# Where row degrees are summed, when one operand tile is loaded, and when projected rows are left for the next layer, in a two-layer Strassen-Winograd graph kernel

## The chip, the cores and the metric

The kernel runs on one core of a Trainium2 chip. The core has a matrix engine (TensorE, PE in the profile; its weight loads are listed as PEld), a vector engine (VectorE, DVE), an activation engine (ScalarE, ACT), GpSimd (POOL) and a sync engine (SyncE, SP). Each works through its own instructions in order, and they wait for each other by semaphores. In this kernel SP issues the large loads, POOL the stores and the loads of rows. The metric is the device time of one execution in microseconds; smaller is better.

## The reference, cut to what matters

```python
def _L0(cur, inc0):                       # N = 4096 rows, D = 512
    head = (inc0 > 0).astype(...)         # head: 1 where the adjacency is positive
    head = head / maximum(sqrt(sum(head * head, axis=-1)), 1e-12)
    inc = inc0 + head
    return (inc @ cur) / sum(inc, axis=-1)
def _L1(X, A, W):
    A2 = A + eye(N)
    dscale = diagonal(A2) ** -0.5
    return relu((dscale[:, None] * A2 * dscale[None, :]) @ (A2 @ X @ W.T))
x = layernorm(x + _L0(x, adj))
x = layernorm(x + _L1(x, adj, L1_gnn_W))
```

All is float32. The adjacency is 4096 x 4096. There are three large products with it: one in layer 0 and two in layer 1. The degree of a row in layer 0 is the row's sum of `inc`, that is the row sum of the adjacency plus the row sum of the normalised head; with c positive entries in the row, the latter is c/sqrt(c) = sqrt(c).

## The kernel before, in words

Every large product is done by a Winograd form of Strassen's scheme: the left factor is cut into four quarters A11, A12, A21, A22, the right one into B11, B21, B22 and one more, and seven products of sums of quarters (with A sums S1 to S4 and B sums T1 to T4) take the place of eight. The seven accumulate in seven PSUM banks; the eighth bank is a spare.

*First stage (layer 0).* Rows are taken in 16 pairs j (row block j and row block j + 16, of 128 rows each). A pair has four chunks c of the contraction (NC = 4), each a tile `a` of 128 x 2048, loaded by SP (`load_chunk`, L308, three buffers) two chunks ahead. For the chunk after the one being multiplied, DVE forms the sums with the head's mask (`prepare1`: L416, L435, L442 and `add_up`, L167 to L170). `multiply1` (L472) then issues 4 x 7 matmuls. B tiles hold W = 258 columns, 256 of features and two of ones, so that products A11, A12 and S1 also give row sums, the degrees; the other four are 256 wide (H). The first pair is done without the scheme (`multiply_plain`, L485). At the start of a pair, `combine` reads the last pair's banks: ACT copies two of them (L503, L507), DVE does the rest (L504 to L513), among it the two columns of `deg`.

The head needs 1/sqrt(count) of a row before its mask. So natural rows of the adjacency go by once more: `load_natural` (SP, L367) brings tiles `nat` of 128 x 512, five buffers, 16 tiles to a pair; `count(k)` has ACT apply Sign to k of them with a sum beside it (L332) and asks for k more loads. `count` is called after each chunk's multiply, with the numbers of a tuple by chunk. `spread(j + 1, 0)`, in the second chunk, reduces the counts on DVE and takes the root on ACT (L336). `layer0` (second chunk) divides by the degree, adds x and normalises (ACT L153 and L162, DVE L159), `operands` (third chunk) forms T sums and POOL stores B operands for the next stage in DRAM (`outer_b[2]`, L540 to L542).

*Second and third stage (layer 1: k = 2 and 3).* Now the order is written out as 224 `steps` (k, s, p, kk): half s of the left rows, product p of an outer seven (`ORDER`), and kk of eight blocks. Each step is seven matmuls of 512 columns (`multiply2`, L278; an inner level of the same scheme), A tiles come two to three steps ahead by SP (`load`, L213 and L217), B operands two groups ahead, a group being two steps (`load_b_up_to`, L250, tile `tr`, three buffers), and DVE sums both (`add_up`, `sum_b` L257 to L259). After eight steps `outer` drains the banks (L684 to L692). The last pair of the first stage is still given to `layer0` in step 0 and `operands` in step 1.

When a half of stage 2 is done, its columns are multiplied with W.T by `project`, two blocks at kk = 2 and 4 of a product, each with seven small products placed between the seven matmuls of a step (`between`, by slot 0 to 6). Each of these uses the spare bank and is copied out by ACT at once (L766 and L768), so the next one waits for this copy. After the seven, DVE forms the results `z` and the difference `t`, and `leave_operands` scales them on ACT by dscale or its negative (L816) and stores them as B operands of stage 3 from POOL (L819, L826); the second half (h = 0) adds T2, T3 and T4 to what the first (h = 1) has written.

Of the kernel before, what the change touches and what calls it, by code (L numbers as in the profile page):

```python
# [13 lines left out]
P = 128  # L14
# [12 lines left out]
def tile_adj_resnorm_d2(  # L27
# [44 lines left out]
    NC = NP // CK  # L72
    CW = CK * P
    W = H + 2
    NAT = 512
    NT = N // NAT
    NQ = NB // 4
# [117 lines left out]
    going = []  # L195
    queue, pairs, later, deferred, raises = [], [], [], [], []

    def fresh():
# [102 lines left out]
    chunks, sums, slots, counts, scale, natural = {}, {}, {}, {}, {}, {}  # L301
    xr = {}

    mask = w1_pool.tile([P, 2, CW], F32, name="mask", bufs=1)
# [65 lines left out]
    def count(times):  # L370
        for _ in range(times):
            if not waiting:
                return
            (j, h, t), nat = waiting.pop(0)
            if j not in counts:
                counts[j] = w1_pool.tile([P, 2, NT], F32, name="cnt")
            signs(nat, nat, counts[j][:, h, t:t + 1])
            load_natural()

    def spread(j, part):  # L380

        if part == 0:
            n = w1_pool.tile([P, 2], F32, name="n", bufs=2)
            nc.vector.tensor_reduce(n, counts.pop(j), axis=mybir.AxisListType.X, op=ALU.add)
            to_scale(n, n)
            scale[j] = n
        elif part == 1:
            n = scale.pop(j)
            nc.vector.tensor_scalar(n, n, EPS, None, op0=ALU.max)
            nc.vector.reciprocal(n, n)  # L390
            d = w1_pool.tile([P, 2, P], F32, name="d", bufs=1)
            for h in range(2):
                nc.vector.tensor_scalar(d[:, h, :], ident, n[:, h:h + 1], None, op0=ALU.mult)
            scale[j] = d
        elif part == 3:

            n = scale.pop(j)
            nc.vector.tensor_scalar(n, n, EPS, None, op0=ALU.max)
            nc.vector.reciprocal(n, n)
            row = dram.tile([P, 2], F32, name=f"sc{j}")  # L400
            nc.gpsimd.dma_start(out=row, in_=n)
            s = w1_pool.tile([P, P, 2], F32, name="sc")
            nc.gpsimd.dma_start(out=s.rearrange("p i h -> p (i h)"), in_=row.rearrange("i h -> (i h)").partition_broadcast(P))
            scale[j] = s.rearrange("p i h -> p h i")
        else:
# [50 lines left out]
        add_up(sums[n], chunks[n])  # L456

    def multiply1(n, acc, then=None):
        c = n % NC
        a, s = chunks.pop(n), sums.pop(n)  # L460
        for i in range(CK):
            kk = c * CK + i
            b = slots[kk]
            cols = slice(i * P, (i + 1) * P)
            if then is not None and i == CK - 1:
                then()
            for m, (left, right, w) in enumerate((
                (a[:, A11, cols], B11, W), (a[:, A12, cols], B21, W), (s[:, S2, cols], T2, H),
                (s[:, S1, cols], T1, W), (s[:, S3, cols], T3, H), (s[:, S4, cols], B22, H),
                (a[:, A22, cols], T4, H),  # L470
            )):
                nc.tensor.matmul(acc[m][:, 0:w], left, b[:, right, 0:w], start=(kk == 0), stop=(kk == NP - 1))  # L472
# [15 lines left out]
    def take(h, acc):  # L488

        y = row_tile("z", 2)  # L490
        nc.scalar.copy(y[:, 0:H], acc[0][:, 0:H])
        nc.scalar.copy(y[:, H:D], acc[1][:, 0:H])
        nc.scalar.copy(deg0[:, h:h + 1], acc[0][:, H:H + 1])
        return y

    def combine(acc):

        q1, q2, q6, q5, q7, q3, q4 = acc
        top, low = row_tile("z", 2), row_tile("z", 2)
        p1, p5 = row_tile("p1", 1)[:, 0:W], row_tile("p5", 1)[:, 0:W]  # L500
        u2, u3 = row_tile("u2", 1)[:, 0:H], row_tile("u3", 1)[:, 0:H]
        deg = small.tile([P, 2], F32, name="deg", bufs=2)
        nc.scalar.copy(p1, q1[:, 0:W])  # L503
        nc.vector.tensor_add(top[:, 0:H], q2[:, 0:H], p1[:, 0:H])  # L504
        nc.vector.tensor_add(deg[:, 0:1], q2[:, H:H + 1], p1[:, H:H + 1])
        nc.vector.tensor_add(u2, q6[:, 0:H], p1[:, 0:H])
        nc.scalar.copy(p5, q5[:, 0:W])  # L507
# [5 lines left out]
        nc.vector.tensor_copy(deg[:, 1:2], p5[:, H:H + 1])  # L513
        return top, low, deg

    def load_rows(j):
        for h in range(2):
# [3 lines left out]

    def layer0(j, C):

        rd = small.tile([P, 2], F32, name="rd", bufs=2)
        nc.vector.reciprocal(rd, C[2])
        stats = []
        for h in range(2):
            y = C[h]
            nc.vector.scalar_tensor_tensor(y, y, rd[:, h:h + 1], xr.pop(h), op0=ALU.mult, op1=ALU.add)
            stats.append(statistics([y]))  # L530
        for h in range(2):
            normalise(C[h], *stats[h])
            nc.gpsimd.dma_start(out=x1_rows[j + h * NP], in_=C[h])

    def operands(j, C):

        top, low, _ = C
# [15 lines left out]
    deg0 = small.tile([P, 2], F32, name="deg", bufs=2)  # L553
# [70 lines left out]
    prepare1(NC)  # L624
    build_last(4)
    multiply_plain(1, 3, low)
    C = top, take(1, low), deg0
    load_rows(0)

    for n in range(NC, NP * NC):  # L630
        j, c = divmod(n, NC)
        if c == 0:
            if j > 1:
                C = combine(acc)
            acc = [bank(m) for m in range(7)]
        if n + 2 >= NP * NC:
            load_up_to(n + 2 - NP * NC)
# [10 lines left out]
            for g in range(5, NP // 2):  # L648
                build_last(g)
        multiply1(n, acc, (lambda: spread(j + 1, 2)) if scales and j == 1 else None)  # L650
        count(((6, 6, 4, 6) if j == 1 else (6, 0, 4, 6))[c])
        if j == 1 and c == 1:
            nc.vector.tensor_scalar(dscale, dscale, 1.0, None, op0=ALU.add)
            nc.scalar.activation(dscale, dscale, AF.Sqrt)
# [46 lines left out]
    def outer(k, p, acc):  # L701
# [26 lines left out]
        else:  # L728
# [6 lines left out]
                into(c21)  # L735
                deferred.append(lambda: add(c11, c21))
            elif p == 6:
                by_way(lambda i, y: add(c21[:, i, :], y))
                deferred.append(lambda: add(c12, c21))
            elif p == 7:  # L740
                by_way(lambda i, y: add(c21[:, i, :], y))
                deferred.append(lambda: less(c22, c22, c21))
            else:
                by_way(lambda i, y: nc.vector.tensor_sub(c21[:, i, :], y, c21[:, i, :]))

    def blocks(h, s):

# [2 lines left out]
    def project(h, s, n, first):  # L750
# [51 lines left out]
        t = row_tile("t", 1, (P, 4, H))  # L802
        for r in range(2):
            nc.vector.tensor_sub(t[:, 2 * r, :], z[r][:, 0:H], z[r][:, H:D])
        for r in range(2):
            leave_operands(h, r * NQ + s * SB + n, z[r], t[:, 2 * r, :], t[:, 2 * r + 1, :])
        yield

    def leave_operands(h, j, z, t, m):

        b = j + h * NP

        def scaled(o, y, by=dscale):
            nc.scalar.activation(o, y, AF.Copy, scale=by[:, b:b + 1])  # L816

        def put(op, y, **how):
            nc.gpsimd.dma_start(out=in_outer(3, j, slice(op, op + 1)), in_=y.unsqueeze(1), **how)  # L819
# [75 lines left out]
    def finish(h, items, acc):  # L895
# [14 lines left out]
        def put(i, op):  # L910
            y = row_tile("y", 2)
            op(y)
            nc.vector.tensor_sub(c21[:, i, :], y, c21[:, i, :])

        def turn(t):
            j, r, cols = items[t]
# [70 lines left out]
    load_up_to(2)  # L987
    load_b_up_to(2)
    sum_b(0)
    C = combine(acc)  # L990
    prepare(1)
    PF = 1
    for n, (k, s, p, kk) in enumerate(steps):
# [104 lines left out]
```

## Time and profile before

| what | value |
|---|---|
| median of 3 runs | 2283.88 us (2283.74 to 2288.45) |
| the profiled execution's own time | 2284.03 us |
| its span, first to last instruction | 2282.1 us |
| mean granted TensorE clock | 0.998 |
| busy: PE / DVE / ACT / POOL | 2255.1 / 1854.4 / 417.3 / 383.3 us |
| first stage by pairs (L472) | from 73.5 to 803.5 us |
| stages 2 and 3 (L278, then L908) | from 803.5 us to the tail at about 2265 us |

In the lists below, a row of a group names the line, the engine, the operation, `tile written<-tiles read`, and the shapes; a row of a timeline begins with its start and its duration in microseconds, and a bracket at its end gives the idle time before it and what ended it. A row of the waits gives the total in microseconds, how often, and the longest. `q` is a PSUM bank, `nat` a tile of natural rows, `tr` the loaded B operands, `ob` and `oa` operands in DRAM. One float32 matmul appears as two records on PE.

### The profile page before, as it was taken

What the parts mean: (1) busy time and instruction counts of PE and PEld (TensorE: products, weight loads), DVE (VectorE), ACT (ScalarE), POOL (GpSimd) and SP (SyncE); (2) the same over time, 40 slices, a digit from 0 to 9 for tenths busy, and PEclk for the clock granted to TensorE, in tenths of its full rate; (3) what the DMA queues carried; (4) which work ended last, traced back from release to release, by engine and by line L of the source; (5) the groups of instructions that cost most, each with busy time, mean ns of one, the idle gap of its engine ahead of it and who ended that gap; (6) DMA issues with size and microseconds to landing.
All of it is one profiled execution on the core that took longest, in us unless ns stands there. A gap on an engine that the chain in (4) does not pass through costs nothing.

```text
span 2282.1 us, 22004 instructions
## 1 busy us (share of the span) xinstructions
PE 2255.1 (99%) x7359; PEld 1380.3 (60%) x7359; DVE 1854.4 (81%) x2619; ACT 417.3 (18%) x991; POOL 383.3 (17%) x548
## 2 busy tenths in 40 slices
PE   8999999999999999999999999999999999999997
PEld 6888888888888844444555444555544444444443
DVE  6988988988988777788876778887666788776788
ACT  4333223332232000000222100122110011100013
POOL 0111112211111110001333300232320000100013
PEclk9999999999999999999999999999999999999999
DMA  9788777878777576575767857576785676766573
GB/s 330 274 287 262 260 233 270 272 262 270 238 240 239 187 266 259 198 283 184 270 240 227 262 209 271 191 283 261 209 256 218 220 258 241 253 238 227 209 269 117
DMA packets 155936, 555.80 MB, mean 244 GB/s; under 512 B 17920, under 2 KB 32272, under 8 KB 117424
## 3 DMA queue, kind: packets, MB, share of 16 engines
q1 hardware_dynamic: 114624, 417.38, 51.6%
q0 software_dynamic: 41200, 137.03, 18.2%
q8 instruction: 58, 0.95, 0.2%
q14 instruction: 54, 0.44, 0.1%
HBM read 434.78 MB, written 119.55 MB: 243 GB/s over the span
## 4 chain that ended last, share of the span: by engine, by line
PE 89%; DVE 5%; DMA 3%; ACT 2%; issue 1%; POOL 0%; SPq 0%; DVEq 0%; ACTq 0%
PE q L278 55%; PE q L472 27%; PE q L766 3%; PE q L485 2%; DMA nat<-adj 2%; DVE s L167 1%; PE q L908 1%; PE q L844 1%; DVE s L169 0%; ACT z L816 0%; ACT nat L332 0%; DVE a L442 0%; DVE mask L435 0%; ACT t L816 0%; DVE ts L257 0%
## 5 line engine op out<-in xcount | busy, mean ns | idle before, releaser
L278 PE MATMUL q<-s,ts 128*128 128x512 f32 x1326 | 612.2, 592 | 0.1
L472 PE MATMUL q<-b,s 128*128 128x256 f32 (+1 forms) x1920 | 454.4, 379 | 0.0
L278 PEld LDWEIGHTS q<-s,ts 128*128 128x128 f32 x1326 | 251.6, 190 | 299.1 <-issue 268.3
L167 DVE TENSOR_TENSOR s<-a 128x1024 f32<-128x1024 f32 x236 | 290.2, 1230 | 161.4 <-PE q L278 131.3
L472 PEld LDWEIGHTS q<-b,s 128*128 128x128 f32 x1920 | 363.1, 189 | 53.1 <-DVE z L510 0.5
L472 PE MATMUL q<-b,a 128*128 128x258 f32 (+1 forms) x1440 | 352.5, 380 | 0.7 <-ACT p L503 0.6
L278 PE MATMUL q<-a,tr 128*128 128x512 f32 x692 | 329.4, 592 | 1.8 <-DMA a<-adj_r 1.8
L472 PEld LDWEIGHTS q<-b,a 128*128 128x128 f32 x1440 | 272.5, 189 | 40.9 <-ACT p L503 1.5
L278 PE MATMUL q<-s,tr 128*128 128x512 f32 x442 | 225.7, 592 | 0.0
L278 PEld LDWEIGHTS q<-a,tr 128*128 128x128 f32 x692 | 129.5, 190 | 145.1 <-issue 138.9
L332 ACT ACTIVATE nat<-nat,tiny 128x512 f32<-128x512 f32 x240 | 170.9, 714 | 235.9 <-DMA nat<-adj 235.7
L278 PE MATMUL q<-a,ts 128*128 128x512 f32 x346 | 176.8, 592 | 0.0
L169 DVE TENSOR_TENSOR s<-a,s 128x512 f32<-128x512 f32 x236 | 167.7, 711 | 8.1
L170 DVE TENSOR_TENSOR s<-a,s 128x512 f32<-128x512 f32 x236 | 167.3, 709 | 8.0
L442 DVE TENSOR_TENSOR a<-a,mask 128x1024 f32<-128x1024 f32 x123 | 150.7, 1225 | 6.6 <-DVE mask L435 0.5
L435 DVE SCALAR_TENSOR_TENSOR mask<-a,sc 128x1024 f32<-128x1024 f32 (+2 forms) x129 | 154.1, 1196 | 2.1
L278 PEld LDWEIGHTS q<-s,tr 128*128 128x128 f32 x442 | 84.0, 190 | 92.1 <-issue 84.6
L684 ACT COPY p<-q 128x512 f32<-128x512 f32 x27 | 15.6, 577 | 631.5 <-PE q L278 631.5
L278 PEld LDWEIGHTS q<-a,ts 128*128 128x128 f32 x346 | 65.7, 190 | 83.0 <-issue 76.1
L425 POOL DMA_DIRECT2D oa<-sr x64 | 57.7, 902 | 283.8 <-DVE sr L416 181.6
L873 POOL DMA_DIRECT2D out<-o x24 | 13.1, 547 | 507.8 <-ACT o L162 507.8
L278 PE MATMUL q<-r,tr 128*128 128x512 f32 x192 | 92.7, 593 | 0.0
(193 smaller groups left out, 2129.4 us busy)
## 6 DMA issues: line engine op xcount, KB each, us to landing
a<-adj_r SPq DMA_DIRECT2D x112, 1024.0 KB, 6.6
a<-oa SPq DMA_DIRECT2D x80, 1024.0 KB, 5.3
nat<-adj SPq DMA_DIRECT2D x240, 256.0 KB, 7.4
a<-adj_q SPq DMA_DIRECT2D x60, 1024.0 KB, 6.2
tr<-ob SPq DMA_DIRECT2D x112, 512.0 KB, 4.0
oa<-sr POOLq DMA_DIRECT2D x64, 512.0 KB, 7.2
oa<-r POOLq DMA_DIRECT2D x32, 1024.0 KB, 9.2
y<-x POOLq DMA_DIRECT2D x64, 256.0 KB, 7.2
```

Of the source, the lines that this page charges most:

```text
L167: nc.vector.tensor_add(s[:, S3:S1 + 1, :], a[:, A11:A22 + 1, :], a[:, A21, :].unsqueeze(1).to_broadcast([P, 2, w]))
L169: nc.vector.tensor_add(s[:, S2, :], a[:, A11, :], s[:, S1, :])
L170: nc.vector.tensor_add(s[:, S4, :], a[:, A12, :], s[:, S2, :])
L278: nc.tensor.matmul(acc[m], left, right, start=(kk == 0), stop=(kk == NQ - 1))
L332: nc.scalar.activation(y, a, AF.Sign, bias=tiny, scale=2.0 ** 64, accum_out=accum)
L425: nc.gpsimd.dma_start(out=dst, in_=sr.rearrange("p m (k i) -> p (m k) i", i=P))
L435: nc.vector.scalar_tensor_tensor(m, v, 0.0, s.unsqueeze(1).to_broadcast(list(v.shape)), op0=ALU.is_gt, op1=ALU.mult)
L442: nc.vector.tensor_add(z, z, y)
L472: nc.tensor.matmul(acc[m][:, 0:w], left, b[:, right, 0:w], start=(kk == 0), stop=(kk == NP - 1))
L485: nc.tensor.matmul(y[:, 0:w], left, slots[kk][:, op, 0:w], start=(kk == 0 and left is k1), stop=(kk == NP - 1 and left is k2))
L766: nc.tensor.matmul(ps, left[:, e, :], wt[:, right, e, :], start=(e == 0), stop=(e == 1))
L844: nc.tensor.transpose(ps[:, at + i * P:at + (i + 1) * P], C_of[3][h][d // 2][:, 2 * r + d % 2, cols], ident)
```

## The change

There are three parts.

1. *Degrees.* From pair 4 on (SUMMED = 4) the three products that gave row sums are 256 wide. Instead, `count` has ACT run over each `nat` tile twice: a copy in place with a sum beside it, then Sign as before. `spread` reduces the sums too (`deg`), and adds the root `n`, which is sqrt(count). `combine` no longer forms `deg` for these pairs. The tiles counted after each chunk are (6, 6, 5, 6) for pair 1 and (5, 4, 5, 2) for the others, where they were (6, 6, 4, 6) and (6, 0, 4, 6).
2. *One load.* At step 1 `load_b_up_to` is not called any more; at step 3 it asks for two groups.
3. *Leaving operands.* For the first of two projected blocks, `leave_operands` is called inside the next step, its two row blocks in slots 2 and 4; for the second it is called at the end of the step as before. T2 and T4 are stored with their sign turned, so that T2 goes with T3 (h = 1) or with T4 (h = 0) in one DMA from one tile. For the two row blocks of a projected block together, six scalings and eight DMAs become four and six where h = 1, and eight scalings and ten DMAs become six and eight where h = 0. The signs are put right where products 6 and 4 are added.

```diff
+    SUMMED = 4
...
             if j not in counts:
                 counts[j] = w1_pool.tile([P, 2, NT], F32, name="cnt")
+                if j >= SUMMED:
+                    totals[j] = w1_pool.tile([P, 2, NT], F32, name="tot")
+            if j >= SUMMED:
+                nc.scalar.activation(nat, nat, AF.Copy, accum_out=totals[j][:, h, t:t + 1])
             signs(nat, nat, counts[j][:, h, t:t + 1])
             load_natural()
...
             to_scale(n, n)
+            if j >= SUMMED:
+
+                deg = degrees[j] = w1_pool.tile([P, 2], F32, name="deg", bufs=3)
+                nc.vector.tensor_reduce(deg, totals.pop(j), axis=mybir.AxisListType.X, op=ALU.add)
+                nc.vector.tensor_add(deg, deg, n)
             scale[j] = n
...
+        wide = W if j < SUMMED else H
...
-                (a[:, A11, cols], B11, W), (a[:, A12, cols], B21, W), (s[:, S2, cols], T2, H),
-                (s[:, S1, cols], T1, W), (s[:, S3, cols], T3, H), (s[:, S4, cols], B22, H),
+                (a[:, A11, cols], B11, wide), (a[:, A12, cols], B21, wide), (s[:, S2, cols], T2, H),
+                (s[:, S1, cols], T1, wide), (s[:, S3, cols], T3, H), (s[:, S4, cols], B22, H),
...
-        count(((6, 6, 4, 6) if j == 1 else (6, 0, 4, 6))[c])
+        count(((6, 6, 5, 6) if j == 1 else (5, 4, 5, 2))[c])
...
-                by_way(lambda i, y: add(c21[:, i, :], y))
+                by_way(lambda i, y: nc.vector.tensor_sub(c21[:, i, :], c21[:, i, :], y))
...
-                by_way(lambda i, y: nc.vector.tensor_sub(c21[:, i, :], y, c21[:, i, :]))
+                by_way(lambda i, y: less(c21[:, i, :], y, c21[:, i, :]))
...
-        for r in range(2):
-            leave_operands(h, r * NQ + s * SB + n, z[r], t[:, 2 * r, :], t[:, 2 * r + 1, :])
+        leaving.extend(lambda r=r: leave_operands(h, r * NQ + s * SB + n, z[r], t[:, 2 * r, :]) for r in range(2))
...
         if h:
-            scaled(m, second, nscale)
-            scaled(z, z)
-            scaled(t, t)
+            scaled(z, dscale)
+            scaled(t, nscale)
             nc.gpsimd.dma_start(out=in_outer(3, j, slice(B21, B22 + 1)), in_=split(z))
-            put(T2, m)
-            put(T3, second)
-            put(T4, t)
+            put(slice(T2, T3 + 1), second)
+            put(slice(T4, T4 + 1), t)
         else:
-            scaled(m, t, nscale)
-            scaled(t, t)
-            scaled(first, first)
-            scaled(second, second, nscale)
-            put(B11, first)
-            put(T1, t)
-            put(T2, m, accum_op=ALU.add)
-            put(T3, second, accum_op=ALU.add)
-            put(T4, m, accum_op=ALU.add)
+            scaled(t, dscale)
+            scaled(first, dscale)
+            scaled(second, nscale)
+            put(slice(T1, T1 + 1), t)
+            put(slice(B11, B11 + 1), first)
+            put(slice(T2, T4 + 1, 2), t, accum_op=ALU.add)
+            put(slice(T3, T3 + 1), second, accum_op=ALU.add)
...
-            nc.vector.tensor_sub(c21[:, i, :], y, c21[:, i, :])
+            less(c21[:, i, :], y, c21[:, i, :])
...
         for pair in going:
             between.update(next(pair))
+        if leaving:
+
+            between[2], between[4] = leaving
+            leaving.clear()
         if n < len(steps) - TAIL:
             multiply2(n, acc, between)
...
-        if n % 2 == 1:
+        if n % 2 == 1 and n > 1:
             load_b_up_to(n // 2 + 3)
...
+        if kk == 6:
+            while leaving:
+                leaving.pop(0)()
```

More of the change, by code (lines that the diff above doesn't have):

```diff
@@ L194, in tile_adj_resnorm_d2 @@
     made = {"a": 0, "s": 0, "load": 0, "load_b": 0}
-    going = []
+    going, leaving = [], []
     queue, pairs, later, deferred, raises = [], [], [], [], []
@@ L300, in tile_adj_resnorm_d2 @@
     nc.gpsimd.memset(ones_f, 1.0)
-    chunks, sums, slots, counts, scale, natural = {}, {}, {}, {}, {}, {}
+    chunks, sums, slots, counts, totals, degrees, scale = {}, {}, {}, {}, {}, {}, {}
     xr = {}
@@ L458, in multiply1 @@
     def multiply1(n, acc, then=None):
-        c = n % NC
+        j, c = divmod(n, NC)
+        wide = W if j < SUMMED else H
         a, s = chunks.pop(n), sums.pop(n)
@@ L492, in take, with combine @@
         nc.scalar.copy(y[:, H:D], acc[1][:, 0:H])
-        nc.scalar.copy(deg0[:, h:h + 1], acc[0][:, H:H + 1])
+        nc.scalar.copy(degrees[0][:, h:h + 1], acc[0][:, H:H + 1])
         return y
-    def combine(acc):
+    def combine(j, acc):
         q1, q2, q6, q5, q7, q3, q4 = acc
         top, low = row_tile("z", 2), row_tile("z", 2)
-        p1, p5 = row_tile("p1", 1)[:, 0:W], row_tile("p5", 1)[:, 0:W]
+        wide = W if j < SUMMED else H
+        p1, p5 = row_tile("p1", 1)[:, 0:wide], row_tile("p5", 1)[:, 0:wide]
         u2, u3 = row_tile("u2", 1)[:, 0:H], row_tile("u3", 1)[:, 0:H]
-        deg = small.tile([P, 2], F32, name="deg", bufs=2)
-        nc.scalar.copy(p1, q1[:, 0:W])
+        nc.scalar.copy(p1, q1[:, 0:wide])
         nc.vector.tensor_add(top[:, 0:H], q2[:, 0:H], p1[:, 0:H])
-        nc.vector.tensor_add(deg[:, 0:1], q2[:, H:H + 1], p1[:, H:H + 1])
+        if j < SUMMED:
+            deg = degrees[j] = w1_pool.tile([P, 2], F32, name="deg", bufs=3)
+            nc.vector.tensor_add(deg[:, 0:1], q2[:, H:H + 1], p1[:, H:H + 1])
         nc.vector.tensor_add(u2, q6[:, 0:H], p1[:, 0:H])
-        nc.scalar.copy(p5, q5[:, 0:W])
+        nc.scalar.copy(p5, q5[:, 0:wide])
         nc.vector.tensor_add(u3, q7[:, 0:H], u2)
@@ L512, in combine @@
         nc.vector.scalar_tensor_tensor(low[:, H:D], u3, -1.0, p5[:, 0:H], op0=ALU.mult, op1=ALU.subtract)
-        nc.vector.tensor_copy(deg[:, 1:2], p5[:, H:H + 1])
-        return top, low, deg
+        if j < SUMMED:
+            nc.vector.tensor_copy(deg[:, 1:2], p5[:, H:H + 1])
+        return top, low
     def load_rows(j):
@@ L524, in layer0 @@
         rd = small.tile([P, 2], F32, name="rd", bufs=2)
-        nc.vector.reciprocal(rd, C[2])
+        nc.vector.reciprocal(rd, degrees.pop(j))
         stats = []
@@ L535, in operands @@
     def operands(j, C):
-        top, low, _ = C
+        top, low = C
         t = row_tile("t", 1, (P, 4, H))
@@ L552, in tile_adj_resnorm_d2 @@
     scale[0] = w1_pool.tile([P, 2, P], F32, name="sc")
-    deg0 = small.tile([P, 2], F32, name="deg", bufs=2)
+    degrees[0] = w1_pool.tile([P, 2], F32, name="deg", bufs=3)
     def load_half(h, c):
@@ L626, in tile_adj_resnorm_d2 @@
     multiply_plain(1, 3, low)
-    C = top, take(1, low), deg0
+    C = top, take(1, low)
     load_rows(0)
@@ L633, in tile_adj_resnorm_d2 @@
             if j > 1:
-                C = combine(acc)
+                C = combine(j - 1, acc)
             acc = [bank(m) for m in range(7)]
@@ L804, in project, with leave_operands, scaled, put @@
             nc.vector.tensor_sub(t[:, 2 * r, :], z[r][:, 0:H], z[r][:, H:D])
-        for r in range(2):
-            leave_operands(h, r * NQ + s * SB + n, z[r], t[:, 2 * r, :], t[:, 2 * r + 1, :])
+        leaving.extend(lambda r=r: leave_operands(h, r * NQ + s * SB + n, z[r], t[:, 2 * r, :]) for r in range(2))
         yield
-    def leave_operands(h, j, z, t, m):
+    def leave_operands(h, j, z, t):
         b = j + h * NP
[L815 to L819, printed above, removed]
+        def scaled(y, by):
+            nc.scalar.activation(y, y, AF.Copy, scale=by[:, b:b + 1])
+        def put(ops, y, **how):
+            o = in_outer(3, j, ops)
+            nc.gpsimd.dma_start(out=o, in_=y.unsqueeze(1).to_broadcast([P, o.shape[1], H]), **how)
         first, second = z[:, 0:H], z[:, H:D]
         if h:
-            scaled(m, second, nscale)
-            scaled(z, z)
-            scaled(t, t)
+            scaled(z, dscale)
+            scaled(t, nscale)
             nc.gpsimd.dma_start(out=in_outer(3, j, slice(B21, B22 + 1)), in_=split(z))
-            put(T2, m)
-            put(T3, second)
-            put(T4, t)
-        else:
-            scaled(m, t, nscale)
-            scaled(t, t)
-            scaled(first, first)
-            scaled(second, second, nscale)
-            put(B11, first)
-            put(T1, t)
-            put(T2, m, accum_op=ALU.add)
-            put(T3, second, accum_op=ALU.add)
-            put(T4, m, accum_op=ALU.add)
+            put(slice(T2, T3 + 1), second)
+            put(slice(T4, T4 + 1), t)
+        else:
+            scaled(t, dscale)
[5 more added lines that the diff above has]
+            put(slice(T3, T3 + 1), second, accum_op=ALU.add)
     def turn_back(ps, at, h, r, cols, fs):
@@ L989, in tile_adj_resnorm_d2 @@
     sum_b(0)
-    C = combine(acc)
+    C = combine(NP - 1, acc)
     prepare(1)
```

## The prediction

> **What bounds the kernel now.** I read the page's busy line first, then what TensorE (PE) waits for, then start-to-start distances of the matmul records, then the timelines around each wait.
>
> ```profile
> PE 2255.1 (99%) x7359; PEld 1380.3 (60%) x7359; DVE 1854.4 (81%) x2619; ACT 417.3 (18%) x991; POOL 383.3 (17%) x548
> ...
> PEclk9999999999999999999999999999999999999999
> ```
>
> PE is busy 99% of the span at an ungated clock (0.998 granted). Busy time alone would not prove a bound, since each record is drawn past the start of the next: a 128x512 record is drawn 592 ns long but the next starts 429 ns later. The starts settle it. The median distance is 429 ns at L278, 215 ns (256 columns) and 217 ns (258) at L472, and in the whole span only 47 distances exceed their median by over 25 ns, 15.4 us together. Everything else is a PE stream with no holes, so the change is worth the columns it takes off plus the holes it closes, less new ones. This is the list of PE's waits:
>
> ```profile
> PE q L343 <- ACT sr L332: 6.7, 3, 6.3
> PE q L766 <- ACT p L768: 4.3, 8, 0.9
> PE q L844 <- DVE c L913: 1.8, 1, 1.8
> PE q L278 <- DMA a<-adj_r: 1.8, 1, 1.8
> PE q L472 <- ACT p L503: 0.6, 1, 0.6
> ```
>
> The first (start) and third (tail) are untouched. The list shows only idle time after the drawn end, so I size each hole by starts, and add the 104 to 105 ns by which a matmul after a hole is late (its weights are no longer loaded ahead).
>
> **The change, part by part.**
>
> *Columns.* From pair 4 on, three of the seven products (L472: A11, A12 and S1) lose two columns. 12 pairs x 16 blocks x 3 = 576 matmuls of two records each, 1152 records. Mean start distance between 125 and 800 us, without holes: 217.55 ns at 258 columns, 215.91 ns at 256. 1152 x 1.64 ns = **1.9 us**, all on the path.
>
> *Degrees from row sums.* ACT gets 192 more activations of 128x512 with a sum. The nearest row is the Sign with a sum beside it (L332, 711 ns, then a 187 ns accumulator read; one starts 705 ns after another), so 0.71 us each, 16 x 0.71 = 11.4 us per pair of 48.5 us. ACT now does about 11.4 us of counting and 4 us of other work per pair, so it fits; what matters is who queues behind it. Here is ACT at a pair boundary:
>
> ```profile
> 548.14 0.71 ACT L332 ACTIVATE nat<-nat,tiny 128x512 f32<-128x512 f32 x1
> 548.76 0.19 ACT L332 ACTIVATION_READ_ACCUMULATOR nat<-nat,tiny 128x1 f32 x1
> 559.25 0.72 ACT L332 ACTIVATE nat<-nat,tiny 128x512 f32<-128x512 f32 x1 [10.30 <-DMA nat<-adj]
> 559.88 0.19 ACT L332 ACTIVATION_READ_ACCUMULATOR nat<-nat,tiny 128x1 f32 x1
> 559.97 0.35 ACT L503 COPY p<-q 128x258 f32<-128x258 f32 x1
> ```
>
> The copy that frees PE's first bank (L503) queues behind the sixth Sign of the last chunk. There are five `nat` buffers, so the sixth tile is loaded only after the chunk load of the same step, and here it took 10.3 us. The new counts (5, 4, 5, 2) never ask for more than five, so every tile was requested a step earlier, and before the boundary ACT has 2 x 1.42 us instead of six Signs. The hole at 559 us goes: 751 ns + 363 ns of slow restarts = **1.1 us**.
>
> The first boundary goes the other way. Pair 1 counts 5 instead of 4 in its third chunk, then still 6. Before, the last of those ten Signs used the first `nat` load after the chunk load (issued 111.42 us, landed 121.36) and L503 ran at 122.16, costing 0.67 us. The eleventh tile stands where the second load after that chunk stood, which landed at 122.97, and adds its own 0.7 us of ACT: L503 moves to about 123.7, **1.5 us lost** (bounds 0 and 2).
>
> In the second chunk four counts (5.7 us) now stand ahead of layer0's square roots (L153), for which VectorE (DVE) waits at L159. They can start after the root at 522.3 us and end by 528 to 530; L153 starts at 533.4 only when DVE's statistics are ready. So this is hidden by DVE's own work; without that cover DVE, which finishes a chunk's sums 3.4 us before PE needs them at that place, would be late next. In `spread` the new `tensor_add` waits for ACT's root of `n` (0.3 us) right after a 0.16 us reduce, where before a 1.2 us addition covered it: 0.5 us of DVE per pair, taken from a lead of about 4.3 us over PE in that chunk; the two removed `deg` operations give back 0.13 us. Nothing on the path.
>
> One rule speaks loudly against this part. The Trainium skill, "ScalarE: Activation LUTs", section "Table sets: the hidden batching unit": changing to a function in another table set reloads the tables, about 2.7 us each time. Alternating a copy with Sign, 32 changes per pair, would be 85 us on top of 27 in a pair of 48.5 us, 12 x 63 = some 750 us slower. But the same section lists copy as filler in every set, and the trace has one single table load (at 0.7 us, 1.28 us long) although the scaled copies at L816 and the roots at L153 alternate in it. I take zero.
>
> *Operand load two steps later.* SP's queue around the start of the second layer-stage:
>
> ```profile
> 803.54 6.35 SPq L217 DMA_DIRECT2D a<-adj_r  x2
> 826.35 0.38 SPq L250 DMA_DIRECT2D tr<-ob  x1
> 826.83 1.04 SPq L217 DMA_DIRECT2D a<-adj_r  x2
> 827.96 0.66 SPq L250 DMA_DIRECT2D tr<-ob  x1
> 828.73 0.75 SPq L217 DMA_DIRECT2D a<-adj_r  x1
> ```
>
> SP stood 16.3 us at the L250 load, which reads what the last pair writes (`ob<-t`, issued 822.87, landed 826.29). Two A loads sat behind it and landed at 835.3 and 837.9; PE had a hole of 1.99 us at 833.0 and 0.45 us of aftermath. Moved, the A loads go as their buffers come free (steps end at about 815 and 821 us) and land by 822 and 828. The moved load still goes at 826 to 829, followed at once by the next `tr`, an A and a resident load; in that crowd it took 6.5 us, so it lands by 836. Its sums take 1.8 us on DVE and PE needs them at step 6, which starts at 839. Hole gone: **2.4 us**.
>
> *First pair's operands.* ACT in the step after such a pair:
>
> ```profile
> 1207.34 0.51 ACT L816 ACTIVATE t<-t,dscale 128x256 f32<-128x256 f32 x1
> 1207.76 0.49 ACT L816 ACTIVATE z<-z,dscale 128x256 f32<-128x256 f32 x1
> 1208.15 0.49 ACT L816 ACTIVATE z<-z,nscale 128x256 f32<-128x256 f32 x1
> 1208.55 0.35 ACT L768 COPY p<-q 128x256 f32<-128x256 f32 x1
> ```
>
> Eight scalings (six in the other half) sit ahead of the copy that frees the spare bank, and the product in slot 3 waits. Eight holes by starts: 456, 487, 905, 902, 445, 486, 1029 and 908 ns = 5.62 us, plus 8 x 104 ns: 6.45 us. Moved into slots 2 and 4 of that step, each row block needs 3 x 0.41 = 1.25 us (2 operations, 1.0 us, in the other half), between product copies 2.58 us apart that take 0.37 us each. Their inputs (L804, done 0.8 to 1.2 us into the step) are ready before slot 2. So all **6.4 us** go.
>
> What is moved with it: 8 DMAs instead of 10 (6 instead of 8) on POOL's queue, about 2.5 us later for the second row block, in one phase behind L237's `oa<-r`. Their readers on SP come two steps later at least. The nearest user is the second pair, which overwrites `z` and `t` at the end of the next step: in the accumulating half the last write landed at 1221.4 and 1283.8 us, against `t` written at 1222.7 and 1284.1. How long do the new last writes take, issued about 7 us into the step? By the skill ("DMA: Bandwidth & Descriptors", "Anatomy of one DMA — SWDGE (gpsimd) path", about 2.0 us + bytes/436e3, an estimate of 2.6 us for 256 KB) they are long done. The trace disagrees: such last writes of a first pair took 8.4 to 10.8 us, of a second pair up to 12.9. By the rows DVE may wait 0 to 2 us there. Cover: the drain of the banks. With two scalings fewer and the hole gone, the copy L684 would end 2.5 us before PE needs bank 0. Cost zero; without the cover up to 1 us at each of four places.
>
> The negations (subtract for add at L738, `less` for subtract at L744 and L913) cost nothing: both kinds take 0.69 us for 128x512.
>
> **Sum** against the profiled execution: 1.9 + 1.1 - 1.5 + 2.4 + 6.4 = 10.3 us. Its span goes from 2282.1 to 2271.8, its own time from 2284.03 (1.9 us outside the span) to 2273.7. That execution is 0.15 us above the median of the runs, 2283.88, so the forecast is **2273.6 us**, 0.45% faster.
>
> **The rivals.** (1) The load hole only moves: `ob<-t` now shares the queues with a 1 MB load, lands late, and the moved `tr` misses step 6. For it: it took 6.5 us and leaves some 2 to 4 us. Against: two loads are out of its way. 2.4 us lost, 2276.0. (2) The products' hole stays: the scalings, still ahead of a copy on the same engine, start late because DVE is late with `t`. For it: DVE is 81% busy. Against: 2 us of room in the slot. 2273.6 + 6.4 = 2280.0, within 0.2% (4.6 us, about what a measurement of this kernel can tell from no change). (3) Slower: the second pair waits for the first pair's accumulating writes. It starts to cost when they land 12 us after issue, and with four places it makes the kernel slower by over 0.2% when each costs (10.3 + 4.6)/4 = 3.7 us, landing about 16 us after issue: 2288.5 or more. The longest in the trace is 12.9.
>
> **How the numbers follow.** Forecast 75%, (1) 12%, (2) 8%, (3) 5%. Faster 0.87, same 0.08, slower 0.05. The forecast's own ends: 2271.5 if the first boundary costs nothing extra, 2278 if the accumulating writes cost 1 us at four places. To hold 8 in 10 I take 2270.5 to 2279.
>
> **What would show it.** No wait of L766 on L768; no PE wait on `a<-adj_r` near 833 us, with two L217 issues between 815 and 822; L472 all 256 wide after pair 3; PE's wait on L503 gone at 559 and about 1.5 us longer at 122. It is wrong if new waits on L503, on L684 or at L472 on DVE appear at many boundaries.

## The result, and the profile after

The changed kernel takes 2281.23 us (median of 20 runs, 2278.84 to 2284.80) against 2285.05 us for the kernel before on the same chip (20 runs, 2283.74 to 2288.45). The ratio is 0.9982, interval 0.9976 to 0.9988. It is faster, by 0.18% and not by the 0.45% of the forecast: about 4 us instead of 10, and 2281.2 us lies above the range (2270.5 to 2279.0).

The profiled execution took 2281.95 us, with a span of 2280.2 us (before: 2284.03 and 2282.1) at a granted clock of 0.998. In the changed kernel the lines are shifted: L279 is the matmul L278 of before, L483 is L472, L514 is L503, L698 is L684, L780 and L782 are L766 and L768, L818 is L804, L829 is L816, and the stores are L833 and L839.

The page's busy lines of the changed kernel:

```profile
PE 2253.3 (99%) x7359; PEld 1380.2 (61%) x7359; DVE 1856.0 (81%) x2619; ACT 535.6 (23%) x1343; POOL 369.4 (16%) x516
...
PEclk9999999999999999999999999999999999999999
```

PE is still the bound. ACT works 118 us more, POOL issues 32 DMAs fewer, and neither tells where the time went. The list of PE's waits does (total us, times, longest):

```profile
PE q L344 <- ACT sr L333: 7.1, 3, 6.2
PE q L854 <- DVE c L713: 1.8, 1, 1.8
PE q L483 <- ACT p L514: 1.6, 1, 1.6
PE q L483 <- DVE s L170: 1.6, 1, 1.6
PE q L279 <- DVE c L699: 1.5, 1, 1.5
PE q L279 <- ACT p L698: 1.3, 4, 0.7
PE q L279 <- DVE u L700: 0.4, 2, 0.2
```

Two lines of before are gone, as forecast: the product's wait for its copy (L780 on L782, eight holes) and the wait for `a<-adj_r` at 833 us. Four lines are new. One, at L483 on DVE L170, is the first row of the table below. The other three are all at L279: on L698, L699 and L700. They stand where `outer` drains the banks after a product. The prediction named a new wait on L684, now L698, as a sign that it is wrong.

Sized by the start-to-start distances of the matmuls, as in the prediction, the holes of the two profiled executions are:

| place | before, us | after, us |
|---|---|---|
| 73 us, DVE L170 (its chunk load landed late) | 0.00 | 1.84 |
| 122 us, first pair boundary, L514 | 0.67 | 2.16 |
| 559 us, pair boundary | 1.11 | 0 |
| 833 us, `a<-adj_r` | 2.44 | 0 |
| eight products of projected blocks | 6.45 | 0 |
| drains at 1163, 1224, 1285 and 1554 us | 0 | 1.21 + 0.58 + 4.42 + 1.17 = 7.38 |

So 10.0 us of holes closed and 10.7 us opened. Holes outside the table, most of them in the first 16 us, add 0.2 us. The columns give about 2 us (0.17 us per pair over twelve pairs), and the last 0.8 us of the 1.9 us by which the spans differ lies in distances too small for this list. The hole at 73 us is in the first pairs, where no part of the change acts. It varies by execution, between 0.3 and 1.8 us in the kernels of the experiments; two of these, with the first stage as before, have 0.6 and 1.1 us.

The places that the prediction showed look as it said. ACT at the pair boundary, in the changed kernel:

```profile
549.41 0.72 ACT L333 ACTIVATE nat<-nat,tiny 128x512 f32<-128x512 f32 x1
550.04 0.18 ACT L333 ACTIVATION_READ_ACCUMULATOR nat<-nat,tiny 128x1 f32 x1
558.93 0.37 ACT L514 COPY p<-q 128x256 f32<-128x256 f32 x1 [8.71 <-PE q L483]
```

ACT stands idle for 8.7 us until PE has finished the bank; nothing is ahead of the copy any more. SP's queue around the start of the second stage:

```profile
803.25 18.35 SPq L218 DMA_DIRECT2D a<-adj_r  x4
830.55 0.89 SPq L251 DMA_DIRECT2D tr<-ob  x2
831.55 0.41 SPq L218 DMA_DIRECT2D a<-adj_r  x1
```

Four A loads now go ahead of the load that waits for the last pair; the two that were late before are issued at 815.27 and 821.28 us. The moved `tr` load, the second of the row, landed at 836.26 us. And ACT in the step after a first projected block:

```profile
1203.77 0.37 ACT L782 COPY p<-q 128x256 f32<-128x256 f32 x1 [3.92 <-PE q L780]
1204.04 0.51 ACT L829 ACTIVATE t<-t,dscale 128x256 f32<-128x256 f32 x1
1204.45 0.50 ACT L829 ACTIVATE z<-z,dscale 128x256 f32<-128x256 f32 x1
1204.85 0.50 ACT L829 ACTIVATE z<-z,nscale 128x256 f32<-128x256 f32 x1
1206.35 0.37 ACT L782 COPY p<-q 128x256 f32<-128x256 f32 x1 [1.00 <-PE q L780]
```

The scalings fit between two product copies, and the second copy still waits for PE, not PE for it.

**Where the new holes come from.** PE at the largest of them, in the timeline of the changed kernel:

```profile
1284.93 1.02 PE L279 MATMUL q<-r,ts 128*128 128x512 f32 x2
1286.61 1.13 PE L279 MATMUL q<-a,tr 128*128 128x512 f32 x2 [0.65 <-ACT p L698]
1289.28 1.75 PE L279 MATMUL q<-a,tr 128*128 128x512 f32 x2 [1.54 <-DVE c L699]
```

A new product wants banks 0 and 1, which `outer` has not drained yet: ACT's copy L698 frees the first, DVE's addition L699 the second. Why are both late? ACT at the same place:

```profile
1283.58 0.51 ACT L829 ACTIVATE t<-t,dscale 128x256 f32<-128x256 f32 x1 [4.94 <-DVE t L818]
...
1285.59 0.50 ACT L829 ACTIVATE z<-z,nscale 128x256 f32<-128x256 f32 x1
1285.99 0.57 ACT L698 COPY p<-q 128x512 f32<-128x512 f32 x1
```

Six scalings of the second projected block stand ahead of the copy, and they began only when DVE had written `t`. And DVE:

```profile
1278.67 0.43 DVE L813 TENSOR_TENSOR z<-u,u 128x256 f32<-128x256 f32 x1 [2.15 <-ACT u L782]
1282.40 0.42 DVE L814 TENSOR_TENSOR z<-p,p 128x256 f32<-128x256 f32 x1 [3.30 <-DMA ob<-z]
...
1283.74 2.29 DVE L245 TENSOR_TENSOR r<-r,a 128x2048 f32<-128x2048 f32 x1
...
1288.54 0.69 DVE L699 TENSOR_TENSOR c<-q,p 128x512 f32<-128x512 f32 x1
```

DVE stood 3.30 us ahead of L814, because the tile `z` that it writes there was still being read by a store of the first projected block. The wait ended when that store landed, at 1282.31 us. All that follows in DVE's queue is late with it: `t`, the 2.29-us sum L245, the sums for the next step (L168 to L171) and L699. DVE's waits of this kind between 1050 and 1690 us:

```profile
DVE z L814 <- DMA ob<-z: 15.4, 6, 3.3
...
DVE z L809 <- DMA ob<-z: 1.7, 2, 1.1
```

The kernel before has no such wait. The stores themselves, from POOL's records of `ob` between 1145 and 1151 us (a first block of the half h = 1), first before and then after, least, median and longest time to landing:

```profile
DMA to landing us min/median/max: 2.2/2.7/3.5
```

```profile
DMA to landing us min/median/max: 4.9/6.8/10.7
```

The first store is issued only 0.8 us later (1146.65 for 1145.83 us) in a stream of steps that itself runs about 3 us ahead of that of before, and the last at 1150.09 for 1149.98 us. But before, all eight went ahead of `oa<-r` (1 MB, POOL's next). Now one `oa<-r` has been issued ahead of them (1146.09 us), a `tr` load goes among them (1148.43 us), and the last one lands 10.7 us after its issue.

### The profile page after: what moved, and what is told of

The parts are those of the page before. It is cut to its first block, busy times and chain, and to the rows that moved or that the text cites. A ratio compares the mean times of both kernels' runs of the same rounds, so it can differ in the third digit from the quotient of the medians.

```text
span 2280.2 us, 22139 instructions
## 1 busy us (share of the span) xinstructions
PE 2253.3 (99%) x7359; PEld 1380.2 (61%) x7359; DVE 1856.0 (81%) x2619; ACT 535.6 (23%) x1343; POOL 369.4 (16%) x516
## 4 chain that ended last, share of the span: by engine, by line
PE 87%; DMA 5%; issue 4%; POOL 2%; DVE 2%; ACT 1%; SPq 0%; DVEq 0%; ACTq 0%; POOLq 0%
PE q L279 51%; PE q L483 31%; PE q L780 3%; DMA nat<-adj 1%; DMA ob<-z 1%; DMA b<-x 1%; DMA ob<-t 1%; PE q L918 1%; DMA a<-adj_q 1%; PE q L854 1%; POOL ob L833 1%; ACT nat L333 0%; POOL oa L238 0%; POOL y L788 0%; POOL y L790 0%
## 5 line engine op out<-in xcount | busy, mean ns | idle before, releaser
L279 PE MATMUL q<-s,ts 128*128 128x512 f32 x1326 | 613.4, 593 | 0.4 <-DVE u L700 0.4
L483 PE MATMUL q<-b,s 128*128 128x256 f32 (+1 forms) x1920 | 453.6, 378 | 1.6 <-DVE s L170 1.6
L279 PEld LDWEIGHTS q<-s,ts 128*128 128x128 f32 x1326 | 252.1, 190 | 300.8 <-issue 270.1
L168 DVE TENSOR_TENSOR s<-a 128x1024 f32<-128x1024 f32 x236 | 290.5, 1231 | 146.4 <-PE q L279 119.1
L483 PEld LDWEIGHTS q<-b,s 128*128 128x128 f32 x1920 | 362.5, 189 | 54.1 <-DVE s L170 2.0
L483 PE MATMUL q<-b,a 128*128 128x256 f32 (+1 forms) x1440 | 350.8, 379 | 1.6 <-ACT p L514 1.6
L279 PE MATMUL q<-a,tr 128*128 128x512 f32 x692 | 330.5, 594 | 2.6 <-DVE c L699 1.5
L483 PEld LDWEIGHTS q<-b,a 128*128 128x128 f32 x1440 | 272.6, 189 | 40.6 <-ACT p L514 2.0
L279 PE MATMUL q<-s,tr 128*128 128x512 f32 x442 | 225.7, 592 | 0.0
L279 PEld LDWEIGHTS q<-a,tr 128*128 128x128 f32 x692 | 129.1, 190 | 147.0 <-issue 135.3
L279 PE MATMUL q<-a,ts 128*128 128x512 f32 x346 | 177.0, 593 | 0.0
L170 DVE TENSOR_TENSOR s<-a,s 128x512 f32<-128x512 f32 x236 | 168.6, 714 | 8.1
L171 DVE TENSOR_TENSOR s<-a,s 128x512 f32<-128x512 f32 x236 | 167.5, 710 | 8.0
L698 ACT COPY p<-q 128x512 f32<-128x512 f32 x27 | 15.6, 577 | 631.5 <-PE q L279 631.5
L452 DVE TENSOR_TENSOR a<-a,mask 128x1024 f32<-128x1024 f32 x123 | 150.7, 1225 | 6.2
L279 PEld LDWEIGHTS q<-s,tr 128*128 128x128 f32 x442 | 84.0, 190 | 92.1 <-issue 83.5
L381 ACT ACTIVATE nat<-nat 128x512 f32<-128x512 f32 x192 | 118.3, 616 | 20.9 <-DMA nat<-adj 20.9
L279 PEld LDWEIGHTS q<-a,ts 128*128 128x128 f32 x346 | 65.5, 190 | 83.7 <-issue 74.6
```

The costliest lines, as they stand in the source:

```text
L168: nc.vector.tensor_add(s[:, S3:S1 + 1, :], a[:, A11:A22 + 1, :], a[:, A21, :].unsqueeze(1).to_broadcast([P, 2, w]))
L170: nc.vector.tensor_add(s[:, S2, :], a[:, A11, :], s[:, S1, :])
L171: nc.vector.tensor_add(s[:, S4, :], a[:, A12, :], s[:, S2, :])
L279: nc.tensor.matmul(acc[m], left, right, start=(kk == 0), stop=(kk == NQ - 1))
L381: nc.scalar.activation(nat, nat, AF.Copy, accum_out=totals[j][:, h, t:t + 1])
L452: nc.vector.tensor_add(z, z, y)
```

## The experiments

**Theory A** is that of the last paragraph: the first block's stores leave late, land later still, and the second block, which writes into the same two `z` buffers and the one `t`, waits for them on DVE. The expectations name the rivals. Every ratio is to the kernel before on the same chip at the same time; 0.001 is 2.3 us.

### Each part alone, put into the kernel before

First, do the parts bring what the sum says? Only the new counts, columns and sums:

> Only the degrees from row sums, in the kernel before. From the two traces: 1.9 us less for the columns, 1.1 us less for the closed hole at 559 us, 1.5 us more at the boundary of pairs 1 and 2: 1.5 us faster than before. Theory A (the loss lies in the moved stores) expects this sum. Theory B (the doubled work of ScalarE disturbs the first stage and is what ate the gain) expects it slower than before by 2 us or more.

Measured: 2284.14 us, ratio 0.9994 (0.9987 to 1.0002). The 559-us hole is gone; the one at 122 us is 1.6 us. Only the load:

```diff
-        if n % 2 == 1:
+        if n % 2 == 1 and n > 1:
             load_b_up_to(n // 2 + 3)
```

> Only the operand load two steps later, in the kernel before. Both theories: the hole near 833 us is gone, 2.4 us faster than before. If the hole only moves to step 6 or 7: within 0.5 us of before, with a wait of TensorE on tr or the sums of it between 839 and 850 us.

Measured: 2283.25 us, ratio 0.9992 (0.9984 to 0.9999). No hole at 833 us, none at step 6. Only the leaving and the turned signs:

> Only the leaving of operands (moved into slots 2 and 4, T2 and T4 negated, stores merged), in the kernel before. Theory A: the eight holes at the products go (6.4 us) and four new ones at the bank drains come (7.4 us in the trace of after), so 0 to 2 us slower than before. Theory B: 6 us faster than before, as the prediction had it.

Measured: 2283.56 us, ratio 0.9990 (0.9984 to 0.9997), 2.3 us faster: neither the 0 to 2 us slower of theory A nor the 6 us faster of theory B. All product holes are gone, worth 6.4 us, but PE waits at the drains after 1169, 1225, 1286 and 1674 us. These holes are 5.0 us together, not 7.4; 1.8 us of the difference is a stretch of slow clock that did not come here (last section). DVE waits at L800 (the L814 of this kernel) as in the full change:

```profile
DVE z L800 <- DMA ob<-z: 13.1, 5, 3.5
```

By the ratios the three parts bring 1.4, 1.8 and 2.3 us, 5.5 together against 4.1 for all at once; each interval is some 1.6 us to either side, so within the noise the parts add up, and no clash between them is seen. The part with the largest term, 6.4 us, brings about a third of it.

### The first block's stores read another tile

The direct test of theory A. In the changed kernel the stores of each first block read from the weights tile `wt`, which nobody overwrites; scalings, number, size and place of the stores stay. A store that no longer reads a scaled tile may leave earlier, though. The third stage's operands from these blocks are thereby not those of the reference.

```diff
-            nc.gpsimd.dma_start(out=in_outer(3, j, slice(B21, B22 + 1)), in_=split(z))
+            nc.gpsimd.dma_start(out=..., in_=wt[:, 0] if other else split(z))
+            if other:
+                t, second = (wt[:, i, 0, :] for i in range(2))
...
+            if other:
+                t, first, second = (wt[:, i, 0, :] for i in range(3))
```

> The changed kernel, with the stores of each first block reading the weight tile instead of z and t: the same number of stores of the same size to the same places in the same order, but the second block need not wait for them to overwrite z and t, and they need not wait for the scalings. What stage 3 multiplies is therefore not the reference's. Theory A (the second block waits to overwrite tiles that are still being stored): no VectorE wait on ob<-z ahead of the second block's z, no wait of TensorE on the drain's first copy near 1163, 1224, 1286 and 1554 us: 5 to 7 us faster than the changed kernel. Theory C (ScalarE and VectorE are simply too busy at the drains, whatever the stores do): the four holes stay, within 1 us of the changed kernel.

Measured: 2273.89 us, ratio 0.9954 (0.9941 to 0.9966), against 0.9982 for the change: 6.4 us less. PE's whole list of waits in this kernel:

```profile
PE q L344 <- ACT sr L333: 6.5, 2, 6.4
PE q L858 <- DVE c L713: 1.9, 1, 1.9
PE q L483 <- ACT p L514: 1.6, 1, 1.6
PE q L483 <- DVE s L170: 1.5, 1, 1.5
PE q L496 <- issue: 0.2, 1, 0.2
```

Nothing at L279 is left: no hole between 128 and 1850 us. At the place with h = 1 shown above the stores kept their times (issued from 1146.53 to 1149.97 us, against 1146.65 to 1150.09; the last one landed 10.7 us after its issue in both), and the drain hole of 1.21 us behind them is gone. So there it is neither their traffic nor POOL's queue that holds PE; it is that the tiles are written again.

In the half h = 0 the stores also left earlier, for no scaling holds them: near 1260 us the last was issued at 1261.19 us, 8.8 us sooner than in the changed kernel, though SP's next `tr` load went only 2.05 us sooner. For those places this run does not part the second writing of the tiles from the earlier stores. The wait that DVE shows there, which ends with the landing of the store, and the next two runs speak for the writing. Theory A holds, and the other terms of the sum come out right together: with this wait gone the kernel stands at the forecast of 2273.6 us.

### How late the stores leave: two slots later, two slots earlier

```diff
-            between[2], between[4] = leaving
+            between[4], between[6] = leaving
```

> The changed kernel with the first block's two row blocks left in slots 4 and 6 of the next step instead of 2 and 4: two slots, 2.6 us later by the distance of the product copies on ACT. Theory A (the second block's z waits for the first block's stores still in flight): VectorE's waits at L814 and L809 on DMA ob<-z, 15.4 + 1.7 us in the changed kernel, longest 3.3, grow by up to 2.6 us at each of eight places, the longest to about 5.9; the holes at the bank drains grow by up to 2.6 us at those four or five places where the changed kernel has them already: 5 to 12 us longer than the changed kernel, ratio to before 1.0005 to 1.0035. Rival (the drain holes come from the four scalings of the second block standing ahead of the copy, whatever the first block does): nothing that the second block issues is altered, so the drain holes stay within 1 us and the ratio is 0.998 to 0.999.

Measured: 2291.75 us, ratio 1.0027 (1.0019 to 1.0035): **slower than before**, as theory A said and its rival excluded. The holes at the drains are 18.1 us, from 7.4; some 4 us of that is slow clock after two of them. DVE's waits between 1050 and 1700 us:

```profile
DVE z L809 <- DMA ob<-z: 20.9, 6, 5.3
DVE z L814 <- DMA ob<-z: 14.3, 6, 3.4
```

The other way:

```diff
-            between[2], between[4] = leaving
+            between[0], between[2] = leaving
```

> The changed kernel with the first block's two row blocks left in slots 0 and 2 of the next step instead of 2 and 4. Theory A: the second row block's stores, the last to land, go about 2.6 us earlier where h = 0, so the longest wait of VectorE on DMA ob<-z falls from 3.3 to about 1 us and the drain holes from 7.4 us to 1 to 2 us; no product hole comes back, since after the slot-1 product there are 2.6 us to the next one: ratio 0.9955 to 0.9965. Rival (the stores queue on POOL and on the DMA engines whatever the slot, so an earlier issue does not land earlier): drain holes stay, ratio 0.998. Second risk: scalings in slot 0 stand ahead of the slot-1 product's copy and VectorE's t is late, so that holes on L780 return at some places, 0.5 to 1 us each: ratio 0.997.

Measured: 2277.01 us (4 runs), ratio 0.9960 (0.9945 to 0.9975). The drain holes are gone entirely, of DVE's waits on `ob<-z` 0.6 us is left, and of the second risk there are two holes at L780, both with h = 1:

```profile
PE q L780 <- ACT p L782: 1.3, 2, 0.7
```

Three placements of the same stores give 0.9960, 0.9982 and 1.0027. How their landing moves is seen at one place, the first block that ends at about 1262 us. Measured against the matmuls, the last store leaves there some 1.8 us earlier and 2.6 us later than in the change. Times from issue to landing of the eight stores, one line each for slots 0 and 2, 2 and 4, 4 and 6:

```profile
DMA to landing us min/median/max: 2.1/4.1/6.2
```

```profile
DMA to landing us min/median/max: 2.1/4.2/12.3
```

```profile
DMA to landing us min/median/max: 2.1/10.1/12.4
```

Later stores also take longer. In the records of these three kernels, a store issued at least 1.7 us ahead of SP's `tr` load (at 1269.77, 1270.52 and 1273.91 us) landed within 6.3 us; of those issued later, one took 4.5 us and all others 9.8 to 12.4 us. With h = 1 the slot hardly moves the stores: near 1146 us they stand behind `oa<-r` in POOL's queue and leave at the same point of the stream, within 0.4 us, in all three. But with slots 0 and 2 the `tr` load went 0.9 us later there, and the last store landed 7.9 us after its issue instead of 10.7. That the load, or the two A loads right behind it, is the cause was not tried.

### The first block left at the end of its own step, stores still merged

```diff
-        leaving.extend(lambda r=r: leave_operands(h, ..., z[r], t[:, 2 * r, :]) for r in range(2))
+        for r in range(2):
+            leave_operands(h, r * NQ + s * SB + n, z[r], t[:, 2 * r, :])
```

> The changed kernel with one thing undone: the first block's operands are left at the end of its own step again, with the merged stores and the negated T2 and T4 kept. Theory A: the drain holes vanish (7.4 us), and because two of the eight or six scalings are gone (0.8 us) the product holes of 0.45 to 1.0 us shrink to some 0.1 us each, 0.5 us together: about 6 us faster than the changed kernel, 9 to 10 us faster than before. Theory B: the product holes return in full, and it is up to 6 us slower than the changed kernel, 2 us or more slower than before.

Measured: 2280.39 us, ratio 0.9978 (0.9971 to 0.9985), only 0.9 us under the change; the larger gain did not come. In the half h = 0 all is as theory A says: no product hole (six scalings instead of eight are enough) and no drain hole. But with h = 1 the product holes are larger than before: 1.04, 2.32 and 1.80 us at 1082, 1143 and 1532 us, and PE ran at half clock after the second.

What differs there is `t`, late on DVE. With two stores fewer per block, POOL reaches three `oa<-r` stores of 1 MB sooner. In this kernel they go at 1102.60 to 1103.67 us, and SP's A load of 1102.94 us, the first of them ahead of it, takes 15.6 us (in the changed kernel 15.1); before, this load went 0.3 us ahead of all three and took 9.2. DVE then waits 3.7 us for it at L237, which it did not before, and has less lead on PE when it comes to `t`. This chain is read from the traces and was not tested by a run, and the merged stores cannot be all of it. In the kernel with the degrees alone, where no store is merged, this load also goes 0.3 us ahead of all three and yet takes 14.6 us; DVE waits 2.2 us for it, and the hole at 1144 us is 1.87 us. What makes these holes larger stays open.

### The two together

So each half got the place that suits it: h = 0 at the end of its own step, h = 1 inside the next.

```diff
+        blocks_left = [lambda r=r: leave_operands(h, ..., z[r], t[:, 2 * r, :]) for r in range(2)]
+        if h:
+            leaving.extend(blocks_left)
+        else:
+            for left in blocks_left:
+                left()
```

> The changed kernel, with the first block's operands left at the end of its own step where they are added (h = 0) and inside the next step as in the change where they are written first (h = 1). In the profile of at_once the h = 0 places had no hole at all, in that of after the first h = 1 place of each half had none. Theory A expects only the drain holes at 1163 and 1554 us to remain (2.4 us of 7.4): 5 us faster than the changed kernel, and no product holes. Theory B (leaving at once always delays the products): four holes of about 0.9 us at the h = 0 products, 1 to 2 us faster than the changed kernel.

Measured: 2275.05 us, ratio 0.9959 (0.9946 to 0.9971), 5.3 us under the changed kernel by the ratios, as expected. No product hole; of the drains 1.7 us is left at 1161 us and some 0.6 at 1550.

### The first pair boundary

```diff
-        count(((6, 6, 5, 6) if j == 1 else (5, 4, 5, 2))[c])
+        count({1: (6, 6, 5, 5), 2: (6, 4, 5, 2)}.get(j, (5, 4, 5, 2))[c])
```

> The changed kernel with the tiles counted after each chunk (6, 6, 5, 5) for pair 1 and (6, 4, 5, 2) for pair 2. The last count ahead of the second pair's boundary then no longer waits for a tile that is loaded behind that step's chunk: the hole near 123 us, 1.8 us and 0.36 us of slow restarts in the profile of after, goes: 2.1 us faster than the changed kernel. If this hole isn't due to the queued count: no change.

Measured: 2280.75 us, ratio 0.9985 (0.9977 to 0.9992). The hole at 123 us, 2.16 us in the change, is gone from the trace, so its cause is as predicted: the eleventh counted tile. In the ratio the expected 2.1 us do not show: the lower end of the interval is only 1.1 us below the change's ratio. The drains cost 7.6 us in this profile, much as in the change, so where the gain went stays open. In faster kernels something of it can be seen. With the last two edits together, and both row blocks of h = 1 in slot 2:

> hybrid and counts together, and where h = 1 both row blocks in slot 2 instead of 2 and 4, so that the stores go 1.7 us earlier. The sum of the two, 7 us faster than the changed kernel, 11 us faster than before; with the earlier stores the holes at 1163 and 1554 us shrink by up to 1.2 us together.

Measured: 2272.99 us (2272.62 to 2275.16, 5 runs), ratio 0.9949 (0.9937 to 0.9962), 7.5 us under the changed kernel. The drain holes did not shrink by the 1.2 us hoped for: 1.7 and 0.5 us are left. And with slots 0 and 2 instead:

> The same with the counts of pairs 1 and 2 changed to (6, 6, 5, 5) and (6, 4, 5, 2). All theories: the hole at 123 us goes, and the time falls by 1.2 to 2.2 us against the kernel with slots 0 and 2.

Measured: 2273.53 us, ratio 0.9945 (0.9929 to 0.9962); 3.5 us under slots 0 and 2 without it by the medians, 2.0 us by the spans (2274.7 and 2272.7), four runs each; 1.2 to 2.2 us was expected. The two product holes with h = 1 are larger here, 1.9 and 1.2 us. Both versions are about 8 us below the changed kernel and 12 below the one before. The second needs only the two edits shown: the slots and the counts.

## Why the prediction was wrong, point by point

*Columns* (1.9 us): right, about 2 us by the trace. ACT's added copies took 0.62 us each and hid beside PE.

*The 559-us hole* (1.1 us): gone, but the size was that of one execution. With the old counts the kernel with the load alone had 0.5 us there and 0.5 at 706 us, and the one with the leaving alone none. *The first boundary* (1.5 us lost): right, 1.49 us between the two profiles, and taking one counted tile away removed the hole. Over all executions it is 0.4 to 1.4 us with the old counts and 1.6 to 2.2 with the new ones.

*The operand load* (2.4 us): right in kind, and 2.4 us between the two profiles. In the two other executions with the old load order (the degrees alone, the leaving alone) this hole was 1.1 us, so 2.4 is near the upper end. No table reload appeared (one table load in the whole execution, as before), and no wait of PE that leads to `spread`.

*The products' holes* (6.4 us): right; all eight went.

*What is moved with it*: **this step failed.** It set the wait of the second pair for the first pair's stores to "Cost zero; without the cover up to 1 us at each of four places". Measured: 7.4 us of holes, and 6.4 us in time when the first block's stores no longer read the tiles that are written again. The mechanism was on the page, as rival (3), and it was mis-sized in four ways.

1. The deadline. The prediction compared the landings with the writing of `t`, at 1284.1 us. But after the change the last store of a row block reads `z`, and `z` is written up to 0.9 us earlier (L800 at 1283.21 us in the profile before). At the place shown above DVE was ready for L814 at 1279.10 us, while the last store had been issued at 1270.02: the wait begins when a store lands 9.1 us after its issue, not 12. It took 12.3.
2. Which places. Only the accumulating half (h = 0) was considered. In the half h = 1 the stores had landed within 3.5 us, and nothing was said of it; moved behind `oa<-r` and in among a `tr` load they took up to 10.7 us and cost 1.21 us at 1163 us and 1.17 at 1554.
3. The cover. "2.5 us before PE needs bank 0" was worked out at one place, near 1222 us, and for ACT's copy alone. At 1285 us DVE's queue also holds the 2.29-us sum L245 and the next step's sums ahead of L699, and a wait of 3.3 us came through to PE as 0.81 us at the first bank and 1.71 us at the second.
4. The clock. In the profiled execution the hole at 1285 us was followed by 1.8 us more because PE ran slow after it (below); these are part of the 7.4 us.

The row for the store's time, 8.4 to 12.9 us, was the right one; the page of the Trainium skill that stood beside it, "DMA: Bandwidth & Descriptors", section "Anatomy of one DMA — SWDGE (gpsimd) path", gives an estimate of 2.6 us, and the measurement decides.

Rival (1) did not happen. Rival (2) gave nearly the measured time, 2280.0 us, by another mechanism: the products' holes did not stay. Rival (3) is what the change with slots 4 and 6 does.

## What to carry to other kernels

When a store is issued later, look for the next writer of the tile it reads, and compare the landing with that instruction's start, tile by tile and place by place; a landing time taken from where the store was is not valid where it will be. Here two slots later turned a gain of 0.2% into a loss of 0.3%, and two slots earlier made it 0.4%, so try the neighbouring slots. A cover must be worked out on every engine that frees a bank, with all that stands in its queue.

## What was not expected of the hardware

After some of the holes PE ran at half speed. Stretches of the changed kernel (PE, PEld, DVE, ACT and POOL busy with counts, then granted clock, DMA share, GB/s):

```profile
1280.00:1285.00 5.00, 5.00 (x13) 2.15 (x12) 2.60 (x5) 1.42 (x4) 0.61 (x2) 1.00 0.33 100
...
1290.00:1293.00 3.00, 3.00 (x5) 1.32 (x4) 2.79 (x5) 0.00 (x0) 1.59 (x3) 0.50 1.01 217
1293.00:1300.00 7.00, 7.00 (x17) 3.04 (x16) 6.86 (x9) 0.00 (x0) 0.55 (x1) 1.00 1.13 337
```

The clock is 0.50 from 1290 to 1293 us, and the records start 853 instead of 429 ns apart: 1.8 us lost, so some 3.6 us at half speed. The holes ahead of it were 0.81 and 1.71 us, with two matmuls between them. The sum of the holes does not decide it. These did the same:

- 0.41 and 1.70 us at the same drain in the kernel with the new counts of pairs 1 and 2 (granted 0.51 from 1287.5 to 1291 us);
- one of 2.32 us in the kernel that leaves the first block at the end of its own step (0.53 from 1146.5 to 1150);
- one of 2.78 us with slots 4 and 6 (0.52 from 1228.5 to 1231.5).

These did not: 1.03 and 1.71 us at the same drain with the leaving alone (1.00 from 1291 to 1295), and one of 2.16 us with slots 4 and 6 (1.00 from 1683 to 1690). The Trainium skill, "TensorE: Matmul & The Clock Gate", Part 1, puts the gating at one idle window of about 3.4 us, its end at one busy window of that length, and calls the window free-running. The length of the slow stretch agrees with that figure, while here 2.1 us of holes were once enough to set it off. That it matters where a hole falls in the window would fit these cases; no run here shows it.
